# Pacing of the last gathers of R in a dense stage: by the matmuls of the stage, or by the transposes and products that follow it

## The chip, the cores and the metric

The kernel runs on one core of a Trainium2 chip. The metric is the device time of one execution in microseconds (us), as the median of several runs. A profile of one execution was taken as well. The engines are called PE (TensorE; its weight loads are PEld), DVE (VectorE), ACT (ScalarE), POOL (GpSimd) and SP (SyncE).

## The reference

The inputs are x (8 batches, 2048 nodes, 128 features) and a symmetric-pattern matrix adj (2048 x 2048) of which about 0.4% is not zero. Two layers follow each other, each with a residual sum and a layer norm:

```
res = si[:, :, None] + sj[:, None, :] + adj * w_r + g_b        # si, sj = x @ parts of g_w
X1  = layernorm(x + einsum('bij,bjd->bid', res, x) @ weight + bias)

x1 = einsum('bnf,nw->bwf', X1, adj);  x2 = 2 * einsum(x1, adj) - X1    # the same adj twice
out = layernorm(X1 + relu(concat([X1, x1, x2, x1, x2]) @ Theta1 + bias))
```

In the first layer the sums with si, sj and g_b have rank 9 and are added by small matmuls; what costs is adj times Y, with Y = w_r * (x @ weight). In the second layer the products with Theta1 are taken first, so that two hops remain: y = X1 @ T1 + adj^T @ U with U = X1 @ T0, and then X1 @ T2 + adj^T @ y.

## The kernel before

The 2048 nodes are 16 chunks of 128. In the first layer the first three chunks (0, 1, 2) are computed densely: for each, PE multiplies the transposed rows of adj (in `wide`) with all sixteen chunks of Y (L862). The thirteen others are computed from lists. While chunks 1 and 2 are multiplied, DVE finds for each of these chunks which of the 2048 nodes have a non-zero entry: one list for each quarter of 32 rows ("quads"), one for each half of 64 and one for the whole chunk, at most 128 nodes in each. Seven lists make one chunk. The order of these chunks is `seq` = 9, 10, 11, 12, 13, 14, 3, 4, 5, 6, 7, 8, 15.

For each list two things are gathered by POOL, in 128 rows, by `gather` (L656 to L666, profile line L659). The first is R: rows of the chunk's columns of adj and of its transpose, 1 KB a row, from `rr_d` into one of four buffers `stage`. The second is Y: rows of 4 KB from `y0_d` (y_d in the profile) into a ring of nine buffers that are named Y in the profile, as are the chunks of Y. A quad set of R has four gathers, the set of halves and whole three. The list `jobs` (L699 to L705) holds the order of all gathers of R: ten quad sets for seq[0] to seq[9], then the set of three for chunk 9, the quads of chunk 7, the set of three for chunk 10, the set of three for chunk 11, and so on.

`gathers(count, mm)` (L709) issues the next `count` of these jobs. With a matmul `mm` each of these gathers waits, by a semaphore, for that matmul. At the start of a set, when three sets are waiting, the oldest is copied by DVE (`keep_r`, L687 and L693) out of its stage buffer into `rc` and `rct`, where the matmuls of listed rows (L894) take their weights. `keep_r` is pinned behind whatever DVE instruction was traced before it. Every gather is tied behind the one traced before it:

```
        if order:
            behind(g, order[-1])
        order.append(g)
```

so POOL's order is the order in which the program is written. The rest is placed by a compile-time scheduler, except what is pinned in program order (SP's loads) or tied behind the last matmul by `in_order` (list `mms`).

In the loop over the dense chunks, `c` is the chunk that is finished and chunk c + 1 is multiplied in sixteen steps j. `finish0` adds x, and `layernorm` gives X1. `make_u` (L388) transposes X1 (PE, L184, eight transposes), copies the transposes (DVE L176, ACT L178), stores X1^T (ACT queue, L396), multiplies it into U (PE, L402, eight products in two halves), copies U (ACT, L407) and stores it (L408). At the end of c = 1 this is done for chunk 0, at the end of c = 2 for chunk 1. Y gathers of chunk 9 (seven) and the first two of chunk 10 are issued at j = 9 to 13 of c = 1, with three gathers of R between them at j = 11.

Then the loop over `seq` begins: the own block of a chunk (L878), `put` (the chunk's R is copied out of its stage buffers), the R gathers of the next chunk, and the listed rows (L894) with the Y gathers that are still missing, each of which waits for its ring buffer.

Of the kernel before, what the change touches and what calls it, by code (L numbers as in the profile page):

```python
# [18 lines left out]
def kernel(  # L19
# [86 lines left out]
    def rows4(name):  # L106
        return w4.tile([P, B, D], F32, name=name, tag="w4")

    def flat(t):
        return t.rearrange("p b f -> p (b f)")  # L110
# [69 lines left out]
    def transpose4(srcs, name, t=None, dve=None, tie=None):  # L180

        pt = p_tr.tile([P, 4, P], F32, name=f"pt_{name}", tag="pt")
        for i, s in enumerate(srcs):
            mm = nc.tensor.transpose(pt[:, i, :], s, ident)  # L184
            if tie is not None:
                tie(mm)
        if t is None:
            t = trp.tile([P, 4, P], F32, name=f"tr_{name}", tag="tr")
        evict(t, pt, dve)
        return t  # L190
# [42 lines left out]
    def load_x(c, name, q, t=None):  # L233
        if t is None:
            t = rows4(f"{name}{c}")
        tc.keep_in_program_order(
            q.dma_start(out=t, in_=x[:, c * P:(c + 1) * P, :].rearrange("b p f -> p b f"))
        )
        return t
# [127 lines left out]
    def acc_pair():  # L367
        par[0] ^= 1
        return bank[2 * par[0]:2 * par[0] + 2]
# [18 lines left out]
    def make_u(c, z, xt, u=None, tie=None, mid=None):  # L388

        for h in range(2):  # L390
            transpose4([z[:, h * HB + i, :] for i in range(4)], f"p{c}_{h}",
                       xt[:, h * HB:(h + 1) * HB, :], tie=tie)
        if mid is not None:
            mid()
        if c < ND:
            nc.scalar.dma_start(out=xt_d[c], in_=flat(xt))  # L396
        if u is None:
            u = rows4(f"u{c}")
        for h in range(2):
            pp = p_sm.tile([P, HB, D], F32, name=f"pp{c}_{h}", tag="sm")  # L400
            for i in range(HB):
                mm = nc.tensor.matmul(  # L402
                    pp[:, i, :], xt[:, h * HB + i, :], th[:, 0, :], start=True, stop=True
                )
                if tie is not None:
                    tie(mm)
            nc.scalar.copy(u[:, h * HB:(h + 1) * HB, :], pp)  # L407
        nc.scalar.dma_start(out=u_d[c * P:(c + 1) * P, :], in_=flat(u))  # L408

    def copy_r(n0, n1):  # L410
        for c in seq[n0:n1]:
            tc.keep_in_program_order(
                nc.sync.dma_start(out=rr_d[c - ND][0:N, 1, :], in_=adj[:, c * P:(c + 1) * P])
            )
# [225 lines left out]
    def tile_lists_end():  # L640
        return lists_end(0, LP, [(h, 0, lists[:, 0:64], 64 * h, NT) for h in range(2)])
# [29 lines left out]
    def gather_r(c, q, m, st, n):  # L671


        gather(
            st[:, n * m * P:(n + 1) * m * P],
            rr_d[c - ND].rearrange("n m f -> n (m f)") if m == 2 else adj128,
            idx if m == 2 else idr,
            4 * c + n if q else (LP + 2 * c, LP + 2 * c + 1, LF + c)[n], NX if m == 2 else N * NC,
        )

    def keep_r(c, q, m, st):

        for o in range(m):
            out = rc[:, c] if o == m - 1 else rct[:, c - ND]
            n, w, o1, a = (4, TW, 0, 0) if q else (2, 2 * TW, P, LP)
            step = m * P + w
            tc.keep_in_program_order(nc.vector.tensor_mul(  # L687
                out[:, o1:o1 + P].rearrange("p (n f) -> p n f", n=n),
                st[:, 0:n * step].rearrange("p (n f) -> p n f", n=n)[:, :, o * P:o * P + w],
                has[:, a + n * c:a + n * c + n][:, :, None].to_broadcast([P, n, w]),  # L690
            ))
            if not q:
                tc.keep_in_program_order(nc.vector.tensor_scalar(  # L693
                    out[:, 2 * P:3 * P], st[:, (2 * m + o) * P:(2 * m + o + 1) * P],
                    has[:, LF + c:LF + c + 1], None, op0=ALU.mult,
                ))
# [12 lines left out]
    def gathers(count, mm=None):  # L709

        for _ in range(count):
            if not jobs:
                break
            c, q, n = jobs.pop(0)
            if n == 0:
                if len(waiting) == 3:
                    keep_r(*waiting.pop(0))
                waiting.append((
                    c, q, int(c >= ND) + 1,
                    stages[:, turn[1] % 4 * BD:turn[1] % 4 * BD + BD + 4 * TW],  # L720
                ))
                turn[1] += 1
            gather_r(*waiting[-1], n)
            if mm is not None:
                tc.add_manual_dep(
                    order[-1].ins, mm.ins.name,
                    mybir.DependencyInfo(
                        mybir.DependencyClass.Sync, mybir.DependencyReason.DATA
                    ), reason="pace",
                )  # L730
# [70 lines left out]
    mms = []  # L801
# [7 lines left out]
    with nc.allow_non_contiguous_dma(reason="512-byte rows of blocks"):  # L809
        pending, accs, xr = None, acc0, load_x(0, "xr", nc.sync)  # L810
        for c in range(ND):
            if c + 1 < ND:
                xr1 = load_x(c + 1, "xr", nc.sync)
            if c == 0:
                more_rows()
                copy_r(2, 9)
                tile_ranks()
                tile_lists()
                half_ranks()
                make_ub()  # L820
                for n in range(NC):
                    tc.keep_in_program_order(
                        nc.sync.dma_start(out=y0_d[n * P:(n + 1) * P, :], in_=flat(Y[n]))
                    )
                copy_r(9, NC - ND)
                tc.keep_in_program_order(nc.sync.dma_start(out=y0_d[N:, :], in_=flat(ub)))
                at = tile_lists_end()
                chunk_ranks()
                rank1(0, accs, si_t(0))
                mm = None  # L830
            else:
                z = finish0(c, accs, xr, c > 1)
            if c + 1 < ND:
                accs1, sit, at1 = acc_pair(), si_t(c + 1), first_at[c + 1]
                for j in range(NC):
                    if c == 0:
                        if j < 2:
                            candidates(2 * j)
                            candidates(2 * j + 1)
                        if j == 2:  # L840
                            z = finish0(c, accs, xr, False)
                            layernorm(z, "0_0", at)
                        if j > 4 and j % 2:
                            list_round((j - 5) // 2)
                    else:
                        if j in (1, 3):
                            list_round((j + 11) // 2)
                        if j == 11:
                            made, at = chunk_lists_end()
                            layernorm(z, "0_1", at)  # L850
                            fetch_own(0, y0_d, seq[0])
                            late0 = fetch_block(0, seq[0])
                    if c == 0:
                        gathers(2, mm)
                    elif j < 3 or j in (11, 14, 15):
                        gathers((2, 2, 1)[j] if j < 3 else 3 if j == 11 else 2, mm)
                    elif 9 <= j < 13:
                        fetch_lists(0, y0_d, seq[0], {9: 2, 10: 4, 12: 7}[j])
                    elif j == 13:
                        fetch_lists(0, y0_d, seq[1], NG4 - 7)  # L860
                    for h in range(2):
                        mm = nc.tensor.matmul(  # L862
                            accs1[h], at1[:, j, :], Y[j][:, h * HB:(h + 1) * HB, :],
                            start=(j == 0), stop=False, skip_group_check=True,
                        )
                        if c == 1 and j == 11:
                            behind(mm, made)
                rank1(c + 1, accs1, sit)
                if c == 0:
                    gathers(3, mm)  # L870
                accs = accs1
            if pending is not None:
                make_u(*pending, tie=in_order)
            pending, xr = (c, z, rows4(f"xt{c}")), xr1

    def block_rows(t, r, accs, start, stop):
# [214 lines left out]
```

## Time and profile before

| what | value |
|---|---|
| median of 3 runs | 855.61 us (852.25 to 860.12) |
| the profiled execution, its own time | 867.91 us |
| its span, first to last instruction | 866.1 us |
| PE busy | 748.5 us (86%) |
| POOL busy | 430.1 us (50%) |
| DVE busy | 364.1 us (42%) |
| gathers of R from rr_d (L659) | 91, mean 1035 ns |
| gathers of Y from y_d (L659) | 203, mean 994 ns |
| DMA, mean over the span | 311 GB/s |

Starts and durations are in us from the first instruction. In a line of the order of time, the brackets give the idle time of the engine ahead of the instruction and what ended it; "issue" is time in which it waited for nothing that the profile shows. In a table by stage, each engine has its busy time and in parentheses its instructions, and the last three columns are PE's granted clock, the DMA engines' busy share and what they moved in GB/s.

### The profile page before, as it was taken

What the parts mean: (1) busy time and instruction counts of PE and PEld (TensorE: products, weight loads), DVE (VectorE), ACT (ScalarE), POOL (GpSimd) and SP (SyncE); (2) the same over time, 40 slices, a digit from 0 to 9 for tenths busy, and PEclk for the clock granted to TensorE, in tenths of its full rate; (3) what the DMA queues carried; (4) which work ended last, traced back from release to release, by engine and by line L of the source; (5) the groups of instructions that cost most, each with busy time, mean ns of one, the idle gap of its engine ahead of it and who ended that gap; (6) DMA issues with size and microseconds to landing.
All of it is one profiled execution on the core that took longest, in us unless ns stands there. A gap on an engine that the chain in (4) does not pass through costs nothing.

```text
span 866.1 us, 10670 instructions
## 1 busy us (share of the span) xinstructions
PE 748.5 (86%) x3546; PEld 373.8 (43%) x3546; DVE 364.1 (42%) x1062; ACT 175.1 (20%) x428; POOL 430.1 (50%) x438
## 2 busy tenths in 40 slices
PE   5899999998829778498996987989999899999994
PEld 4666665643324333153344442333343444445541
DVE  5555667769523335155353010000100046555666
ACT  3665664010011212021222000000000002011111
POOL 0000000277466676657675456766655656566660
PEclk9999999999869998799998999999999999999998
DMA  8699997799968889979997889999998989999994
GB/s 283 194 306 309 342 303 215 231 373 398 287 212 264 268 274 322 368 250 344 342 363 259 280 314 349 315 341 394 383 365 307 322 290 372 350 341 354 342 350 155
DMA packets 177548, 269.19 MB, mean 311 GB/s; under 512 B 17698, under 2 KB 127701, under 8 KB 175438
## 3 DMA queue, kind: packets, MB, share of 16 engines
q0 software_dynamic: 50400, 151.21, 49.0%
q1 hardware_dynamic: 103900, 90.02, 32.0%
q10 hardware_dynamic: 23186, 27.20, 8.8%
q8 instruction: 30, 0.49, 0.2%
q14 instruction: 32, 0.26, 0.1%
HBM read 246.75 MB, written 62.55 MB: 357 GB/s over the span
## 4 chain that ended last, share of the span: by engine, by line
PE 53%; DMA 19%; issue 10%; another core or an unknown queue 8%; POOL 3%; DVE 3%; ACT 2%; POOLq 1%; SPq 0%; DVEq 0%; ACTq 0%
PE acc L894 19%; DMA Y<-u_d,idx 9%; DMA Y<-y_d,idx 9%; PE acc L862 7%; PE acc L878 5%; PE acc L342 4%; PE acc L332 4%; PE acc L952 3%; POOL Y L659 3%; PE pt_a L184 2%; PE pp L402 2%; DMA rc<-in_adj_dram 1%; PE pt_x L184 1%; PE pt_r L970 1%
## 5 line engine op out<-in xcount | busy, mean ns | idle before, releaser
L659 POOL DMA_INDIRECT Y<-y_d,idx x203 | 201.8, 994 | 134.7 <-PE acc L894 72.4
L894 PE MATMUL acc<-Y,rc 128*32 128x512 f32 (+2 forms) x896 | 222.3, 612 | 21.9 <-DMA Y<-u_d,idx 11.7
L659 POOL DMA_INDIRECT stage<-rr_d,idx x91 | 94.2, 1035 | 199.8 <-PE rank_c L514 164.4
L659 POOL DMA_INDIRECT Y<-u_d,idx x112 | 111.4, 994 | 69.8 <-PE acc L894 35.5
L894 PEld LDWEIGHTS acc<-Y,rc 128*32 128x32 f32 (+2 forms) x896 | 59.5, 129 | 174.5 <-issue 107.0
L894 PE MATMUL acc<-Y,rct 128*32 128x512 f32 (+2 forms) x364 | 106.2, 621 | 18.6 <-issue 14.0
L878 PE MATMUL acc<-Y,rd 128*128 128x512 f32 x148 | 70.0, 594 | 0.8 <-issue 0.8
L894 PEld LDWEIGHTS acc<-Y,rct 128*32 128x32 f32 (+2 forms) x364 | 25.5, 129 | 90.4 <-issue 67.5
L862 PE MATMUL acc<-Y,wide 128*128 128x512 f32 x128 | 59.9, 620 | 4.3 <-issue 4.3
L383 DVE TENSOR_TENSOR xs<-acc,xs 128x512 f32<-128x512 f32 x26 | 17.8, 684 | 103.8 <-PE acc L894 59.8
L176 DVE COPY z<-acc 128x512 f32<-128x512 f32 x9 | 6.2, 692 | 115.7 <-issue 41.0
L219 ACT ACTIVATE st<-st,epst 128x8 f32<-128x8 f32 x32 | 10.0, 311 | 210.1 <-DVE st L218 112.8
L184 PE MATMUL pt_a<-ident,rc 128*128 128x128 f32 x256 | 37.6, 282 | 6.4 <-DMA rc<-in_adj_dram 6.0
L972 DVE SCALAR_TENSOR_TENSOR z<-z,pt_r 128x512 f32<-128x512 f32 x32 | 20.5, 684 | 47.0 <-PE acc L894 28.5
L862 PEld LDWEIGHTS acc<-Y,wide 128*128 128x128 f32 x128 | 24.7, 199 | 34.5 <-issue 34.4
L311 DVE TENSOR_REDUCE stage<-rct 128x64 f32<-128x2048 f32 x13 | 29.7, 2286 | 23.1 <-ACT rct L178 23.1
L332 PE MATMUL acc<-wx,tr_x 128*128 128x130 f32 x256 | 36.5, 286 | 3.2 <-ACT tr_x L178 2.8
L303 DVE TENSOR_REDUCE rc<-rc 128x64 f32<-128x2048 f32 x16 | 36.5, 2278 | 6.3 <-DMA rc<-in_adj_dram 6.3
L332 PEld LDWEIGHTS acc<-wx,tr_x 128*128 128x128 f32 x256 | 32.8, 194 | 13.4 <-ACT tr_x L178 5.9
L184 PEld LDWEIGHTS pt_a<-ident,rc 128*128 128x128 f32 x256 | 30.9, 145 | 16.3 <-issue 14.7
L342 PE MATMUL acc<-Y,wide 128*128 128x512 f32 x64 | 36.0, 645 | 1.7 <-ACT Y L336 0.5
L407 ACT COPY u<-pp 128x512 f32<-128x512 f32 x30 | 17.5, 585 | 98.3 <-PE acc L894 58.7
(221 smaller groups left out, 895.2 us busy)
## 6 DMA issues: line engine op xcount, KB each, us to landing
rc<-in_adj_dram SPq DMA_DIRECT2D x16, 1024.0 KB
rr_d<-rct SPq DMA_DIRECT2D x13, 1024.0 KB
rr_d<-in_adj_dram SPq DMA_DIRECT2D x13, 1024.0 KB
xs<-in_x_dram SPq DMA_DIRECT2D x21, 512.0 KB
y_d<-Y SPq DMA_DIRECT2D x16, 512.0 KB
out_dram<-z ACTq DMA_DIRECT2D x16, 512.0 KB
u_d<-u ACTq DMA_DIRECT2D x15, 512.0 KB
Y<-y_d SPq DMA_DIRECT2D x15, 512.0 KB
```

Of the source, the lines that this page charges most:

```text
L184: mm = nc.tensor.transpose(pt[:, i, :], s, ident)
L303: nc.vector.tensor_reduce(mk[:, c, :], a.rearrange("p (w f) -> p w f", f=TW), AX.X, ALU.max, apply_absolute_value=True,)
L311: nc.vector.tensor_reduce(mkt[:, :, 4 * c:4 * c + 4], at.rearrange("p j (t f) -> p j t f", f=TW), AX.X, ALU.max, apply_absolute_value=True,)
L332: nc.tensor.matmul(py[:, i, 0:D + 2], xt[b // HB][:, (b + i) % HB, :], wx, start=True, stop=True,)
L342: nc.tensor.matmul(acc0[h], first_at[0][:, c, :], Y[c][:, h * HB:(h + 1) * HB, :], start=(c == 0), stop=False, skip_group_check=True,)
L383: nc.vector.tensor_add(xr[:, hs, :], accs[h], xr[:, hs, :])
L659: g = nc.gpsimd.indirect_dma_start(out=out, out_offset=None, in_=src, in_offset=bass.IndirectOffsetOnAxis(ap=ids[:, n:n + 1], axis=0), bou ...
L862: mm = nc.tensor.matmul(accs1[h], at1[:, j, :], Y[j][:, h * HB:(h + 1) * HB, :], start=(j == 0), stop=False, skip_group_check=True,)
L878: in_order(nc.tensor.matmul(accs[h], r, t[:, h * HB:(h + 1) * HB, :], start=start, stop=stop, skip_group_check=True,))
L894: in_order(nc.tensor.matmul(accs[h][w * t:w * t + w], r[:, o + w * t:o + w * t + w], gs[t][:, h * HB * D:(h + 1) * HB * D], start=False, s ...
L952: in_order(nc.tensor.matmul(accs[h][:, b, :], x1t[c][:, h * HB + b, :], th[:, i, :], start=(b == 0), stop=False, skip_group_check=True,))
L972: nc.vector.scalar_tensor_tensor(z[:, hs, :], z[:, hs, :], 0.0, pt, op0=ALU.max, op1=ALU.add)
```

## The change

In the step c = 1 the gathers of R at j = 14 and j = 15 (two each, waiting for a dense matmul) are taken out. After each `make_u` in this loop, that is for chunk 0 and for chunk 1, four gathers of R are issued: two wait for the last of the eight transposes (`mms[-9]`), two for the last product of U (`mms[-1]`). So eight gathers stand where four stood; the four that are added here are taken from the next chunks' sets, which issue four fewer later on.

```
@@ -852,8 +852,8 @@
                     if c == 0:
                         gathers(2, mm)
-                    elif j < 3 or j in (11, 14, 15):
-                        gathers((2, 2, 1)[j] if j < 3 else 3 if j == 11 else 2, mm)
+                    elif j < 3 or j == 11:
+                        gathers((2, 2, 1)[j] if j < 3 else 3, mm)
                     elif 9 <= j < 13:
                         fetch_lists(0, y0_d, seq[0], {9: 2, 10: 4, 12: 7}[j])
@@ -871,6 +871,8 @@
             if pending is not None:
                 make_u(*pending, tie=in_order)
+                gathers(2, mms[-9])
+                gathers(2, mms[-1])
             pending, xr = (c, z, rows4(f"xt{c}")), xr1
```

More of the change, by code (lines that the diff above doesn't have):

```diff
@@ L854 @@
                         gathers(2, mm)
-                    elif j < 3 or j in (11, 14, 15):
-                        gathers((2, 2, 1)[j] if j < 3 else 3 if j == 11 else 2, mm)
+                    elif j < 3 or j == 11:
+                        gathers((2, 2, 1)[j] if j < 3 else 3, mm)
                     elif 9 <= j < 13:
@@ L873 @@
                 make_u(*pending, tie=in_order)
+                gathers(2, mms[-9])
+                gathers(2, mms[-1])
             pending, xr = (c, z, rows4(f"xt{c}")), xr1
```

## The prediction

> **What bounds the kernel now.** I read the page first, then the chain of waits over 195 to 330 us, then the order of time of each engine around the place of the change, and last the table by stage.
>
> ```profile
> span 866.1 us, 10670 instructions
> PE 748.5 (86%) x3546; PEld 373.8 (43%) x3546; DVE 364.1 (42%) x1062; ACT 175.1 (20%) x428; POOL 430.1 (50%) x438
> L659 POOL DMA_INDIRECT stage<-rr_d,idx x91 | 94.2, 1035 | 199.8 <-PE rank_c L514 164.4
> ```
>
> No engine is full over the whole span, so the stage decides. The 91 gathers of R (tile stage) are issued one at a time by POOL. The chain shows what the end of the dense stage hangs on:
>
> ```profile
> 224.65 10.21 PE acc L862 x20
> 240.15 16.55 another core or an unknown queue
> 257.56 4.11 PE pp L402 x16
> 261.67 3.48 PE acc L878 x8
> 265.14 5.64 PE acc L894 x28
> ```
>
> The reader is to see that dense matmuls (L862) lead until 235, that in this execution something takes 16.55 us out of the chain, and that the U of chunk 1 (L402), the own blocks (L878) and the first listed rows (L894) follow. POOL is not in the chain here. The order of time on POOL and PE:
>
> ```profile
> 229.64 0.99 POOL L659 DMA_INDIRECT Y<-y_d,idx  x1 [6.70 <-issue]
> 234.84 1.00 POOL L659 DMA_INDIRECT stage<-rr_d,idx  x1 [0.30 <-issue]
> 238.76 1.00 POOL L659 DMA_INDIRECT Y<-y_d,idx  x1 [0.30 <-issue]
> 245.26 1.01 POOL L659 DMA_INDIRECT stage<-rr_d,idx  x1 [0.30 <-issue]
> 247.88 1.00 POOL L659 DMA_INDIRECT stage<-rr_d,idx  x1 [0.30 <-issue]
> 250.50 1.00 POOL L659 DMA_INDIRECT stage<-rr_d,idx  x1 [0.31 <-issue]
> 253.11 1.00 POOL L659 DMA_INDIRECT stage<-rr_d,idx  x1 [0.30 <-issue]
> 258.23 1.12 POOL L659 DMA_INDIRECT stage<-rr_d,idx  x1 [4.12 <-DVE rc L687]
> 267.25 0.99 POOL L659 DMA_INDIRECT Y<-y_d,idx  x1 [5.23 <-PE acc L894]
> 236.70 1.09 PE L184 MATMUL pt_p<-ident,xr 128*128 128x128 f32 x8
> 238.21 2.05 PE L402 MATMUL pp<-th,xt 128*128 128x128 f32 x16 [0.42 <-DVE xt L176]
> 240.10 1.04 PE L184 MATMUL pt_p<-ident,xr 128*128 128x128 f32 x8
> 255.26 0.59 ACT L407 COPY u<-pp 128x512 f32<-128x512 f32 x1 [7.91 <-remote]
> 250.00:255.00 5.00, 0.00 (x0) 0.00 (x0) 0.00 (x0) 0.00 (x0) 3.19 (x4) 0.50 0.27 76
> ```
>
> From 229.64 to 254.11 POOL issues 19 gathers in a row, each 1.00 us with 0.30 us ahead of it: 1.30 us a gather. "Issue" there means that no semaphore held it. So POOL is bound by its own issue, not by the waits that pace it. The first wait of another kind is at 267.25, where a Y gather waits for a listed-rows matmul that frees its buffer. The last line (busy time by engine, clock, DMA share, GB/s) shows the DMA engines at 0.27 and PE idle at half clock.
>
> **What the Trainium skill says.** "DMA: Bandwidth & Descriptors", section "Anatomy of one DMA — SWDGE (gpsimd) path": DMA engines do not wait on semaphores, the wait sits on the issuing sequencer. So a paced gather holds everything behind it on POOL; the trace agrees, POOL stands 5.23 us before 267.25. "Perfetto Trace Analysis", section "DMA Instruction — SWDGE (GPSIMD)": the profiled end of such a DMA is when its descriptors are written, not when data has landed; so 1.00 us is issue alone, and the semaphore record for the gather issued at 250.50 shows the landing at 253.07, 2.57 us on. The same DMA page, "Queues, rings and completion order": each DMA engine takes the queues in turn, packet by packet; late R gathers thus share with row loads; no view here separates that share. "TensorE: Matmul & The Clock Gate", "What's actually happening": after an idle window of about 3.4 us the array runs at half clock; the table shows 0.50 from 250 to 255.
>
> **The change, part by part.** Number the gathers of R by chunk: R7 (4, quads), R10 (3), R11 (3). Before: R7 at j = 14 and 15, paced by dense matmuls; R10 after the own blocks of chunk 9 begin; R11 one step later. After: R7 in two pairs, behind X1^T and behind U of chunk 0; then R10 and the first R11 in two pairs, behind X1^T and U of chunk 1; two R11 remain.
>
> 1. *POOL's order.* Every gather is tied behind the one traced before it, so the order on POOL is the traced order. Before: 5 Y, R7 x4, R10 x3, R11 x3, Y of chunk 10. After: the same list. No gather is added or removed, none overtakes a Y. Cost 0.
>
> 2. *The old waits.* The two dense matmuls end before 235; R7 begins at 245.26. They held nothing: gain 0.
>
> 3. *The new waits, PE in time.* X1^T of chunk 0 ends at 236.70 + 1.09 = 237.8; U of chunk 0 at 238.21 + 2.05 = 240.3; X1^T of chunk 1 at 240.10 + 1.04 = 241.1. U of chunk 1, without the hole of 16.55 us, follows after two copies of X1^T; with 0.84 us from copy to first matmul (256.72 to 257.56), 2.05 us of matmuls as for chunk 0, and an estimate of 0.6 us for the second copy behind ACT's queue (one 0.59 us copy), it ends at 241.1 + 0.84 + 2.05 + 0.6 = 244.6. POOL reaches the four pairs at 245.26, 247.88, 250.50 and 253.11 for the first of each. Slack 7.5, 7.6, 9.4 and 8.5 us. Nothing waits. Cost 0; the cover is the run of Y gathers ahead, and it would be gone if PE ran 8 us late.
>
> 4. *The new waits, PE late as in this execution.* ACT's second copy of U of chunk 0 starts at 255.26 when its matmuls count as done, and U of chunk 1 ends at 257.56 + 4.11 = 261.67. Then R7's third goes at 255.3 instead of 247.88, its fourth at 256.6, R10's first two at 257.9 and 259.2, its third waits for 261.7, R11 follow at 263.0, 264.3 and 265.6, and POOL is free at 265.6 + 1.0 + 0.3 = 266.9. Behind it is the Y gather of chunk 10, which before could not go until 267.25 because of the listed rows. Slack 0.3 us: delay 0. This holds whenever PE is late, because four gathers (5.2 us) run against PE's own 3.48 us of own blocks plus its first listed rows, 261.67 to 267.12 = 5.45 us.
>
> 5. *Who needs the late R.* R10 is copied by DVE (L687, L693) for chunk 10 at 276.27; its last gather, issued at 261.7, would land with the 4.7 us that the gather of 258.23 took (262.89) at 266.4. Ten us of cover. R11 is used a chunk later, R7 much later. Cost 0.
>
> 6. *DMA load.* In case 4 two to three R gathers (at most 128 rows of 1 KB, 0.13 MB each) move from before 264 to the stretch in which Y of chunk 10 lands. 0.39 MB at the page's mean of 311 GB/s is 1.3 us; the engines are 66 to 88% busy there, so the bounds are 0 and 1.3 us on Y. PE waits for these Y at 279 to 286, so it can reach the path. I take 0.7.
>
> 7. *DVE and the buffers.* Each new set makes the oldest of three waiting sets be copied out. One set of quads moves from DVE's idle time at 230.3 to behind the copy of X1^T at 238.2: two instructions, about 0.2 us apart, 0.4 us on the statistics of chunk 2, whose product is not transposed until 270.6. The other two stay behind the copy of X1^T of chunk 1, as at 257.43. Cost 0, upper bound 0.4. SP's loads and ACT's stores are neither moved nor added. A wait word on POOL costs some 0.05 us under a running gather.
>
> *Sum.* PE in time: 0. PE late: +0.7 (0 to 1.7). Against the profiled execution's own 867.91 us (span 866.1 and 1.8 around it) that is 867.9 to 869.6. It carries the hole and lies 12.3 us above the median of the runs, 855.61; the change in us is carried over to the median unchanged, since neither case scales with the run.
>
> **Rivals.** *The waits bind but are hidden* (step 4): 855.6 + 0.7 = 856.3. For it: the profiled hole. Against: it needs PE more than 7.5 us behind POOL.
>
> *Slower: the last wait backs up into chunk 10.* If U of chunk 1 is late and POOL's remaining gathers take longer than 1.30 us each (one at 276.36 took 1.48), the Y of chunk 10 starts late. Price: with six R gathers still ahead when POOL is let go, 6 x 1.30 = 7.8 instead of 5.45 us gives +2.4; six R of 0.13 MB in front at 311 GB/s give +2.5; and when the PE gaps at 279 to 286 join into one over 3.4 us, half clock adds up to the 4.1 - 2.05 = 2.1 us per 16-matmul U and likewise for listed rows, an estimate of 4 to 5 us for one chunk. Together about +9.4: 865. It decides from a Y start later than 268 on. Against it: step 4's race comes out even by construction.
>
> *Faster: less traffic beside the Y of chunks 9 and 10 and the stores of X1^T and U.* At most 7 x 0.13 MB at 311 GB/s = 2.9 us: 852.7; a fall past 1% would also need the compiler's plan, which sees the R later, to place the untied DVE and ACT work better: 846 as an estimate. Against: the stretch 250 to 255 has the DMA engines at 0.27, so there is no queue to relieve, and the hole starts at 240.15, before the first R at 245.26.
>
> **How the numbers follow.** Nothing binds: 0.58, 855.6. Binds and is hidden: 0.22, 856.3. Backs up: 0.13, 865. Faster: 0.07, 846. The two likeliest differ by less than can be measured (about 1%), so one figure: 856. Faster by over 1% 0.07, within 1% 0.80, slower by over 1% 0.13. The range holds the two middle cases, the 0 to 1.7 us of step 6 and 7, the spread of the runs (852.25 to 860.12), and reaches to the backed-up case: 849 to 865.
>
> **What would show it.** Right: POOL's list in the same order, R7 starting some 16 us after the first Y gather, with "issue" ahead of R7 and R10, or, with PE late, a wait on PE L184 or L402 ahead of them and the first Y of chunk 10 still waiting on PE L894. Wrong: that Y gather starting right behind an R gather at "issue" after a POOL wait on L402, listed rows of chunk 10 waiting longer for Y, or a POOL order other than the one listed.

## The result and the profile after

Beside each other on one chip, the kernel before takes 859.24 us (852.25 to 866.30) and the kernel after 855.05 us (851.62 to 861.47), medians of 20 runs each. The ratio on record is 0.9975, with an interval of 0.9952 to 0.9998: 0.25% faster, some 2 us, where no change was forecast (856, range 849 to 865). The two medians lie 4.2 us apart, so the size is known only roughly. The gain is smaller than the 1% that the chances speak of, and about as large as what the kernel before later strays from itself (1.0021), so this comparison alone doesn't settle that there is one. Ratios are of fast runs, and the profiled execution before (867.91 us) is a slow one, but a fast one of the same kernel (e5_control below, 861.27 us) has the same hole.

The profiled execution after took 853.63 us, with a span of 851.9. Its page:

```profile
span 851.9 us, 10671 instructions
PE 754.3 (89%) x3546; PEld 374.6 (44%) x3546; DVE 364.4 (43%) x1062; ACT 174.8 (21%) x428; POOL 427.3 (50%) x438
L659 POOL DMA_INDIRECT stage<-rr_d,idx x91 | 92.5, 1016 | 198.2 <-PE rank_c L514 163.9
```

The same number of instructions on every engine, the same 91 gathers of R. Nothing was saved in work, so a gain has to come from waits. The chain of waits of the kernel after, in the stretch of which the prediction showed five lines (line numbers are two higher than before: L896 is the old L894, L880 the old L878):

```profile
220.18 9.42 PE acc L862 x20
235.66 5.69 another core or an unknown queue
242.21 2.05 PE pp L402 x8
244.26 4.79 issue
249.04 2.08 PE pp L402 x8
251.12 4.01 PE acc L880 x8
255.13 4.79 PE acc L896 x26
```

Before, one piece of 16.55 us stood between the dense matmuls and U of chunk 1. After, there are two, 5.69 and 4.79 us. In the order of time of POOL, PE, DVE and ACT the place looks so (the brackets: idle before, and what ended it); the last line is from the table by stage:

```profile
229.25 0.99 POOL L659 DMA_INDIRECT Y<-y_d,idx  x1 [6.78 <-ACT xr L225]
244.84 1.00 POOL L659 DMA_INDIRECT stage<-rr_d,idx  x1 [0.30 <-issue]
250.07 1.00 POOL L659 DMA_INDIRECT stage<-rr_d,idx  x1 [0.31 <-issue]
255.07 0.99 POOL L659 DMA_INDIRECT stage<-rr_d,idx  x1 [2.70 <-PE acc L880]
260.27 1.00 POOL L659 DMA_INDIRECT Y<-y_d,idx  x1 [0.30 <-PE acc L896]
231.44 1.09 PE L184 MATMUL pt_p<-ident,xr 128*128 128x128 f32 x8
233.17 0.30 DVE L687 TENSOR_TENSOR rct<-stage,has 128x128 f32<-128x128 f32 x1
241.37 0.69 DVE L176 COPY xt<-pt_p 128x512 f32<-128x512 f32 x1 [5.71 <-remote]
254.74 0.58 ACT L407 COPY u<-pp 128x512 f32<-128x512 f32 x1 [5.75 <-PE acc L880]
250.00:255.00 5.00, 5.00 (x14) 2.54 (x12) 0.00 (x0) 0.26 (x1) 2.00 (x2) 0.78 0.43 150
```

R7 starts at 244.84 with "issue" ahead of it, so its waits bind nothing here. The third gather of R10 stands 2.70 us for U of chunk 1. Y of chunk 10 follows R11 without a gap. PE, which had no busy time from 250 to 255, now fills these 5 us. From the first transpose of chunk 0 (231.44) to the end of U of chunk 1 (251.12) it is 19.7 us; before it was 236.70 to 261.67, 25.0 us. Below, this length is called the stretch. One thing in these lines is easily read over: in the profile after, the stretch ends at 251.12, before POOL's first wait for PE begins (255.07 - 2.70 = 252.37), and DVE's copy of X1^T of chunk 1 comes at 241.37 in the middle of POOL's run. So that wait didn't make the stretch of this pair shorter; what did is open.

### The profile page after: what moved, and what is told of

Same layout as the page of the kernel before. It is cut to its first block, busy times and chain, and to the rows that moved or that the text cites. A ratio compares the mean times of both kernels' runs of the same rounds, so it can differ in the third digit from the quotient of the medians.

```text
span 851.9 us, 10671 instructions
## 1 busy us (share of the span) xinstructions
PE 754.3 (89%) x3546; PEld 374.6 (44%) x3546; DVE 364.4 (43%) x1062; ACT 174.8 (21%) x428; POOL 427.3 (50%) x438
## 4 chain that ended last, share of the span: by engine, by line
PE 54%; DMA 25%; issue 11%; POOL 4%; ACT 3%; DVE 1%; another core or an unknown queue 1%; POOLq 1%; SPq 0%; DVEq 0%; ACTq 0%
PE acc L896 19%; DMA Y<-y_d,idx 13%; DMA Y<-u_d,idx 10%; PE acc L862 7%; PE acc L880 6%; PE acc L342 4%; PE acc L954 4%; PE acc L332 4%; POOL Y L659 3%; PE pp L402 2%; PE pt_a L184 2%; DMA rc<-in_adj_dram 1%; PE pt_x L184 1%; PE pt_p L184 1%; PE pt_r L972 1%
## 5 line engine op out<-in xcount | busy, mean ns | idle before, releaser
L896 PE MATMUL acc<-Y,rc 128*32 128x512 f32 (+2 forms) x896 | 226.5, 608 | 18.7 <-issue 7.6
L896 PEld LDWEIGHTS acc<-Y,rc 128*32 128x32 f32 (+2 forms) x896 | 59.2, 128 | 175.7 <-issue 113.7
L896 PE MATMUL acc<-Y,rct 128*32 128x512 f32 (+2 forms) x364 | 108.5, 625 | 26.4 <-issue 13.1
L880 PE MATMUL acc<-Y,rd 128*128 128x512 f32 x148 | 72.0, 610 | 0.0
L896 PEld LDWEIGHTS acc<-Y,rct 128*32 128x32 f32 (+2 forms) x364 | 27.0, 130 | 96.2 <-issue 71.5
```

The costliest lines, as they stand in the source:

```text
L880: in_order(nc.tensor.matmul(accs[h], r, t[:, h * HB:(h + 1) * HB, :], start=start, stop=stop, skip_group_check=True,))
L896: in_order(nc.tensor.matmul(accs[h][w * t:w * t + w], r[:, o + w * t:o + w * t + w], gs[t][:, h * HB * D:(h + 1) * HB * D], start=False, s ...
```

## The experiments

The theory that stood after this comparison: the waits give the gain, by something that they do to the late results of PE (theory W). Rivals: DVE's moved copy gives it (theory D); it is chance (theory N). Every kernel ran beside the kernel before on the same chip. The five sets differ in one thing that turned out to matter: what the kernel before itself took.

| set | before, us | kernel | ratio (95%) | stretch, us | POOL's first pause, us | PE's results from, us |
|---|---|---|---|---|---|---|
| record | 859.24 | before | | 25.0 | 254.11 | 256.72 |
| | | after | 0.9975 (0.9952 to 0.9998) | 19.7 | 252.37 | 254.74 |
| first | 830.55 | e1_order | 1.0010 (0.9991 to 1.0028) | 12.5 | | |
| | | e2_waits | 0.9994 (0.9969 to 1.0020) | 9.7 | | |
| | | e3_hold | 1.0018 (1.0003 to 1.0033) | 8.3 | | |
| | | e4_again | 0.9991 (0.9972 to 1.0009) | 14.9 | | |
| second | 863.87 | e5_control | 1.0021 (0.9997 to 1.0045) | 23.7 | 254.45 | 256.12 |
| | | e6_again | 0.9916 (0.9892 to 0.9940) | 14.9 | 242.25 | 245.51 |
| | | e7_waits | 0.9988 (0.9960 to 1.0016) | 21.8 | 249.90 | 252.31 |
| | | e8_early | 1.0017 (0.9991 to 1.0042) | 25.7 | 249.41 | 252.35 |
| third | 858.37 | e9_order | 1.0025 (1.0003 to 1.0048) | 23.0 | 250.64 | 253.08 |
| | | e10_r7 | 0.9976 (0.9941 to 1.0012) | 16.9 | 246.97 | 249.05 |
| | | e11_y | 0.9988 (0.9956 to 1.0020) | 22.2 | 248.20 | 249.24 |
| | | e12_late | 1.0005 (0.9979 to 1.0031) | 18.0 | 248.72 | 250.66 |
| fourth | 862.63 | e13_sp | 0.9937 (0.9906 to 0.9967) | 14.3 | 243.65 | 245.55 |
| | | e14_again | 0.9950 (0.9925 to 0.9974) | 17.9 | 247.23 | 249.40 |
| | | e15_r7 | 1.0006 (0.9974 to 1.0038) | 15.0 | 242.40 | 244.39 |
| | | e16_both | 1.0000 (0.9970 to 1.0029) | 16.0 | 244.88 | 247.19 |
| fifth | 830.92 | e17_hold | 1.0005 (0.9983 to 1.0028) | 12.2 | | |
| | | e18_again | 1.0032 (1.0006 to 1.0058) | 10.4 | | |

The pause is the first idle time of POOL over 1 us after the first Y gather: the start of the gather behind it less the idle time in its bracket. The last column is the start of DVE's first step on results of PE behind the pause (in the profile after, where DVE's came earlier, ACT's copy of U). By this definition the last column lies behind the pause; what the table can show is how close behind, and that it moves with the pause. Against it stand late results that came while POOL was still issuing, in at least ten of the fourteen profiles: the first half of U of chunk 0 in seven of them, 0.8 to 10.4 us ahead of the pause (246.76 in the kernel before), and three copies in the profile after. Stretch, pause and copy are of one profiled execution each; the ratios are of many runs.

**First set: the parts of the change.** e1_order is the change without its waits:

```
-                gathers(2, mms[-9])
-                gathers(2, mms[-1])
+                gathers(2)
+                gathers(2)
```

> The changed kernel without its waits: the eight gathers of R stand after U of chunks 0 and 1, tied to no matmul. POOL's order and DVE's order are those of the changed kernel, so only one copy of a quad set is moved on DVE and no wait is added. If the waits bring the 0.25%, the ratio to before is 1.000 (within 0.002). If the moved copy on DVE brings it, 0.9975. If the difference measured was chance, 1.000. In its profile POOL runs from the first Y gather to the last R gather without a stop but for the stage buffers (R11 waiting for DVE).

e2_waits is the kernel before with only the waits of R10 and R11's first gather:

```
             make_u(*pending, tie=in_order)
+            if c == 2:
+                gathers(2, mms[-9])
+                gathers(2, mms[-1])
```

> The kernel before with the waits alone: R7 stays at j = 14 and 15 with its dense matmuls, and R10 with the first R11 stands after U of chunk 1, two behind its X1^T and two behind its U. The copies on DVE stay where they were before. If the waits bring the 0.25%, 0.9975; if the moved copy brings it, 1.000; if chance, 1.000. In its profile POOL stops ahead of the third R10 until U of chunk 1 is done, as in the changed kernel (2.70 us there).

e3_hold puts eight gathers behind U of chunk 1 (`if c == 2: gathers(8, mms[-1])` in place of the two calls):

> All eight gathers of R wait for the last product of U of chunk 1. If a POOL that stands still lets PE finish X1^T and U sooner, the stretch from the first transpose of chunk 0 to the last U of chunk 1 shrinks from 24.97 us (before) and 19.7 us (changed) to about 13 us, nearly what the matmuls and copies need. Behind that U POOL then has ten gathers of R (13 us) ahead of the Y of chunk 10, against 5.45 us of PE's own work: Y starts about 7.6 us later than PE could use it. Relief theory: the two offset, 0.995 to 1.003. Back-up rival without relief: up to 7.6 us slower, 1.005 to 1.009.

e4_again is the kernel after:

> The changed kernel once more, beside the others on the same chip: 0.9975 if its gain is real (interval 0.9952 to 0.9998 so far), 1.000 if it was chance.

All four are within 0.2% of before, the whole change too (e3_hold is 0.18% slower, with an interval that just leaves out 1). The trace shows why. In e1_order neither copy of U of chunk 1 is late, in the order of time of ACT:

```profile
235.63 0.58 ACT L407 COPY u<-pp 128x512 f32<-128x512 f32 x1 [4.20 <-PE pp L402]
242.25 0.58 ACT L407 COPY u<-pp 128x512 f32<-128x512 f32 x1 [0.77 <-PE pp L402]
```

The last product of U of chunk 1 is done at 242.2, before POOL comes to R7 at 245.64; no wait for it could have bound. The longest stretch of the set, 14.9 us in e4_again, holds one late copy, for which PE waits 5.11 us, and ends before R7 as well. POOL issues its gathers at the same times as in the profiled kernel before, yet PE's results come promptly. That is the case "PE in time" of the prediction's step 3, and it gives what step 3 says, nothing. The kernel before takes 29 us less here than beside the result: this set could not show the gain at all.

**Second set: PE is late again.** e5_control is the kernel before; e6_again the kernel after; e7_waits is e2_waits again. e8_early brings R7 forward into POOL's idle time ahead of the first Y gather:

```
-    sets = [(c, True) for c in seq[:10]]
+    sets = [(c, True) for c in seq[:11]]
-        if n in (0, 2, 4):
+        if n in (2, 4):
-                    elif j < 3 or j in (11, 14, 15):
-                        gathers((2, 2, 1)[j] if j < 3 else 3 if j == 11 else 2, mm)
+                    elif j < 5 or j == 11:
+                        gathers((2, 2, 1, 2, 2)[j] if j < 5 else 3, mm)
```

> The kernel before, unchanged, against itself. Every theory expects a ratio of 1 with an interval of about 0.002 to each side; its middle shows how far a comparison strays with no change at all. Its trace is read for one thing: whether the stretch from the first transpose of chunk 0 to the end of U of chunk 1 is long (25 us, as in the profiled kernel before) or short (8 to 15 us, as in the four kernels of the first set).

> The kernel after, again. If the gain of 0.25% comes from the waits while PE is late, it appears (0.996 to 0.999) where this run's stretch is long and POOL waits for U of chunk 1 (2.70 us in the profile after), and not where the stretch is short (0.999 to 1.001). If it comes from the copy that DVE does later, it appears in both. If it was chance, the ratio is within 0.002 of 1 whatever the stretch.

> The kernel before, with R7 paced by the dense matmuls as it was, and only the four gathers behind make_u of chunk 1 tied to the transposes and the products of U. If the wait for U of chunk 1 gives the gain, this has all of it where PE is late: 0.996 to 0.999. If DVE's order gives it, this has none: 1.000.

> The kernel before with the four gathers of R7 at j = 3 and 4 of the step c = 1, ahead of the Y gathers, in the 6 us in which POOL stood idle before the first Y gather (5.96 us at 230.06 in the first set's profile of the order alone). Theory that POOL's issue bounds the first listed chunks: the ten gathers ahead of the first free Y gather of chunk 10 become six, that Y starts up to 4 x 1.30 = 5.2 us sooner, and the kernel is 2 to 5 us faster (0.994 to 0.998). Rival, that the Y gather waits for its buffer, which the listed rows of chunk 9 free, or that the R of later chunks only moves the wait: 0.999 to 1.001. If the earlier R holds up the first Y gathers behind it, 1.002 or more.

e5_control has the hole of the kernel before again:

```profile
257.63 1.00 POOL L659 DMA_INDIRECT stage<-rr_d,idx  x1 [3.18 <-DVE rc L687]
256.12 0.69 DVE L176 COPY xt<-pt_p 128x512 f32<-128x512 f32 x1 [15.26 <-remote]
```

The control strays to 1.0021, and the kernel after gains 0.84%: theory N falls. e7_waits has little or none of it. e8_early, which should have helped a POOL-bound chunk 10, gains nothing. The traces of this set gave the theory that the rest of the study tests. First the kernel after (e6_again), the order of time of POOL and DVE:

```profile
246.04 1.00 POOL L659 DMA_INDIRECT stage<-rr_d,idx  x1 [3.79 <-remote]
251.83 1.00 POOL L659 DMA_INDIRECT stage<-rr_d,idx  x1 [3.48 <-PE pp L402]
237.77 0.21 DVE L221 RECIPROCAL st<-st 128x8 f32<-128x8 f32 x1 [2.99 <-issue]
245.51 0.69 DVE L383 TENSOR_TENSOR xr<-acc,xr 128x512 f32<-128x512 f32 x1 [3.47 <-remote]
```

Here R7's waits do bind, twice. POOL has issued gathers without a break since 216.45 and stands still from 242.25; 3.3 us later the first result of PE arrives at DVE. During POOL's run the hand-over between DVE and ACT in the layer norm is slow as well: L221 waits 2.99 us for ACT where the kernel before has 0.38. The delay thus lies in part ahead of the stretch, which begins at 241.66 here and at 235.31 in e7_waits: U of chunk 1 ends at 256.52, only 0.6 us sooner than in e7_waits (257.07), though the stretch is 6.9 us shorter and no gain of e7_waits is shown. Now e8_early, DVE and POOL:

```profile
230.76 0.21 DVE L630 TENSOR_SCALAR rct<-pl 128x48 f32<-128x48 f32 x1 [11.18 <-remote]
252.35 0.69 DVE L383 TENSOR_TENSOR xr<-acc,xr 128x512 f32<-128x512 f32 x1 [13.32 <-remote]
260.81 1.00 POOL L659 DMA_INDIRECT stage<-rr_d,idx  x1 [11.40 <-DVE rc L687]
```

Filling POOL's idle 6 us came with a second wait, 11.18 us where the profiled kernel before has 4.51 (without this move e15_r7 has 9.03, so the move isn't shown to be its cause), and the old one ends 2.9 us after POOL's pause (260.81 - 11.40 = 249.41). Hence theory P: where PE's results are late, they come when POOL stops issuing gathers, and the waits of the change make it stop sooner.

**Third set: theory P.** e9_order is e1_order again. e10_r7 has the calls behind `make_u` under `if c == 1`, so only R7 waits. e11_y takes j = 12 and 13 out of the lists fetched in step c = 1 and has, behind `make_u` of chunk 0:

```
+                if c == 1:
+                    n = len(order)
+                    fetch_lists(0, y0_d, seq[0], 7)
+                    fetch_lists(0, y0_d, seq[1], NG4 - 7)
...
+                        order[n].ins, mms[-9].ins.name,
```

e12_late is the kernel before without the calls at j = 14 and 15 and with the later quad sets at `n in (3, 5, 7)`, no wait added.

> The kernel after without its waits: the same order on every engine, four gathers behind make_u of chunk 0 and of chunk 1, none of them waiting for PE. Theory P (a pause of POOL): what PE, DVE and ACT signal to each other arrives late for as long as POOL issues gathers without a break, and the waits of R7 break that run early, at about 242 to 245 us instead of 250 to 254. Then this has none of the gain: 0.998 to 1.002, and on a chip where PE is late, its first results after the run come 2 to 3 us after POOL's first pause, not before 250 us. Theory D (DVE's order): all of the gain, 0.992 to 0.997. On a chip where PE is not late, both give 1.000.

> The kernel after with the four gathers behind make_u of chunk 0 alone (R7, waiting for X1^T and U of chunk 0), and nothing behind make_u of chunk 1. Theory P, where PE is late: all of the gain of the whole change, 0.991 to 0.998, with POOL waiting for PE ahead of R7 (3.79 us in the second set's run of the kernel after). If the gain needs the second wait too, 0.998 to 1.000. Where PE is not late: 1.000.

> The kernel after with the pause put earlier: the last three Y gathers of chunk 9 and the two of chunk 10 are moved behind make_u of chunk 0 as well, and the first of them waits for its transposes. Theory P, where PE is late: POOL pauses at about 237 to 239 us instead of 242 to 245, chunk 0's results come some 5 us sooner, and U of chunk 1 ends before 250 us: 0.988 to 0.994, better than the kernel after. Rival: Y of chunk 9 now comes late and the listed rows of chunk 9 wait for it by what the pause takes, 2 to 4 us: 1.000 to 1.004; on a chip where PE is not late this rival is what theory P expects too, at 1.000 to 1.002.

> The kernel before with the four gathers of R7 left out of this place, without any wait on PE: R7 follows three sets later (and the quads of chunks 6 and 8, or what stands there in the list, likewise), when POOL is past the stage. POOL's unbroken run is four gathers, 5.2 us, shorter. Theory P, where PE is late: PE's results after the run come about 5 us sooner (251 instead of 256 us), 0.994 to 0.998. Theory that only a wait on PE helps: 0.999 to 1.001. Where PE is not late: four gathers fewer ahead of Y of chunk 10 are worth 0 to 3 us there and are paid back later, 0.997 to 1.001.

e9_order speaks between W and D. Order of time, POOL, ACT and DVE:

```profile
254.87 0.99 POOL L659 DMA_INDIRECT stage<-rr_d,idx  x1 [4.23 <-DVE rc L687]
253.02 0.59 ACT L407 COPY u<-pp 128x512 f32<-128x512 f32 x1 [6.42 <-remote]
253.08 0.69 DVE L176 COPY xt<-pt_p 128x512 f32<-128x512 f32 x1 [13.90 <-remote]
```

Every engine has the order of the kernel after, no gather waits for PE, PE is late, and there is no gain (1.0025). That speaks against D, but the kernel after itself didn't run in this set; the fourth set completes it. POOL pauses first at 250.64, and both copies start 2.4 us later. In e12_late, POOL and DVE:

```profile
252.81 1.00 POOL L659 DMA_INDIRECT stage<-rr_d,idx  x1 [4.09 <-DVE rc L687]
250.66 0.69 DVE L176 COPY xt<-pt_p 128x512 f32<-128x512 f32 x1 [8.95 <-remote]
```

Here no PE wait is added and POOL's run is only shorter: the pause moves to 248.72, the copy to 250.66, the stretch to 18.0 us, as P says, and yet the time is 1.0005. e11_y missed its aim: the transposes of chunk 0 were not late in its profile (POOL first stood at 248.20), and the time did not move. e10_r7 lies where the whole change lay at first, with an interval that holds 1.

**Fourth set: POOL's issue or the bytes.** e13_sp loads R7 and R10 by SP's queue instead of by POOL. The loads take as many rows, but not those of the lists, so only its time can be compared:

```
+        if (c, q) in ((seq[10], True), (seq[1], False)):
+            load = tc.keep_in_program_order(nc.sync.dma_start(
+                out=st[:, n * m * P:(n + 1) * m * P],
+                in_=rr_d[c - ND].rearrange("n m f -> n (m f)")[n * P:(n + 1) * P],
+            ))
...
+            return
```

e14_again is the kernel after, e15_r7 is e10_r7, and e16_both joins the kernel after with e12_late's later sets (`gathers(1, mms[-1])` in the second call).

> The kernel before, but the seven gathers of R7 and R10 are plain loads of the same 128 rows of 1 KB each by SP's queue, the first of them waiting for the last Y gather in front to land; the rows are not those of the lists, so the products of these two sets are not the reference's. Bytes and buffers stay, POOL's unbroken run ends with the second Y gather of chunk 10, at about 245 us. Theory P (POOL's issue): where PE is late, the copies of U of chunk 0 and of X1^T of chunk 1 come at 246 to 248 us instead of 252 to 257, 1 to 3 us after POOL's pause. Theory T (the transfers): POOL's pause changes nothing, the copies come when the R loads have moved, from 252 us on. Time: P 0.994 to 0.999, T 0.999 to 1.003; SP's own loads stand behind the R loads, which may cost 1 to 3 us in either case.

> The kernel after, again. Theory P: 0.991 to 0.998 where the stretch of the kernels without waits is long, with POOL waiting for PE at R7 or at R10; 0.999 to 1.001 where it is short.

> R7's waits alone, again. Theory P with the first pause deciding: the same ratio as the kernel after of this set within 0.002. If the second wait, for U of chunk 1, adds to it: 0.002 or more behind the kernel after, and 1.000 if it gives all.

> Both: R7 follows three sets later, R10 waits for X1^T and U of chunk 0 (two gathers and one), R11 for X1^T and U of chunk 1. POOL's first pause is where the kernel after has it, and four gathers fewer stand ahead of Y of chunk 10. If POOL's issue is what chunk 10 waits for, 0.003 better than the kernel after of this set; if its Y waits for the listed rows of chunk 9, as 1.70 us on PE L896 in the second set's run of the kernel after says, the same as that kernel within 0.002.

e13_sp is faster by 0.63%. POOL and DVE, and two lines of its table by stage (busy time by engine, PE's clock, DMA share, GB/s):

```profile
252.25 1.00 POOL L659 DMA_INDIRECT stage<-rr_d,idx  x1 [8.60 <-DVE rc L700]
245.55 0.69 DVE L176 COPY xt<-pt_p 128x512 f32<-128x512 f32 x1 [1.29 <-remote]
243.00:246.00 3.00, 0.00 (x0) 0.00 (x0) 1.68 (x4) 0.39 (x1) 0.66 (x1) 0.58 0.86 294
246.00:249.00 3.00, 2.71 (x12) 2.71 (x13) 2.19 (x13) 0.78 (x2) 0.00 (x0) 0.50 0.74 300
```

POOL pauses at 243.65 and the copy starts at 245.55, while the DMA engines are at 0.86 and move 294 GB/s; the R loads are issued only at 248.67. In the kernel before it was the reverse: from 250 to 255 the DMA engines were at 0.27, POOL was issuing for most of it, and the results were still out. In e5_control they were out at 0.80 (245 to 250) and in e9_order at 0.26 (247 to 250). So the load of the DMA engines is not what holds PE's results. POOL's issue, or something that goes with it, fits; the transfers of the gathers themselves go with it, and no run separates the two. As in e12_late, no wait on PE was needed to shorten the stretch. The 0.63% can't be put down to that alone, since POOL also has seven gathers less to issue.

The kernel after gains 0.50% in this set. R7's wait alone (e15_r7) and both waits with R7 placed later (e16_both) gain nothing, although their stretches, 15.0 and 16.0 us, are shorter than the 17.9 of the kernel after. That speaks against a simple sum in which each us of the stretch reaches the end. e15_r7 also tells on D: it has DVE's moved copy, behind the copy of X1^T of chunk 0 (244.39), and no gain in a set in which the kernel after has one:

```profile
244.99 0.28 DVE L687 TENSOR_TENSOR rct<-stage,has 128x128 f32<-128x128 f32 x1
```

So D falls: the moved copy by itself gives no gain. But e16_both has both waits and no gain either, so theory W isn't shown: waits and a shorter stretch aren't enough.

**Fifth set.** e17_hold is e3_hold and e18_again the kernel after.

> The kernel of e3_hold again: nothing behind make_u of chunk 0, eight gathers behind make_u of chunk 1, all waiting for the last product of its U. Where PE is late, theory P: POOL pauses with the last Y gather at about 244 us and stays still until U of chunk 1, which ends 250 us or sooner, the shortest stretch of all kernels; if a shorter stretch is what the time follows, 0.991 to 0.996. Rival: all ten gathers then stand ahead of Y of chunk 10, which starts 13 us after U of chunk 1, later than the listed rows of chunk 9 (5.5 us) would let it, and gives the gain back: 0.998 to 1.004. Where PE is not late: 1.002, as measured in the first set.

> The kernel after, again, as the yardstick of this set: 0.991 to 0.998 where the stretch of 15 us or more is seen, 0.999 to 1.001 where it is 8 to 13 us.

The kernel before takes 830.92 us here, the stretches are 12.2 and 10.4 us, and the question put to this pair could not be answered: there was no lateness to shorten. What it adds is the other side: with PE in time the kernel after is not faster (1.0032, with an interval just above 1; 0.9991 in the first set).

## Why the prediction was wrong, step by step

- **Steps 1 and 2 held.** POOL's list is the same, and the old waits held nothing. But one line was misread ahead of them: "the first wait of another kind is at 267.25" passes over the gather of 258.23, ahead of which POOL stands 4.12 us, from 254.11, for a copy of DVE. It is beside this pause that PE's late results come (255.26 and 256.72).
- **Step 3 held where it applies.** With PE in time nothing binds. Against a predicted 0, one set measured 0.9991, and the other 1.0032, some 2.7 us slower and just clear of 1; the kernel before has strayed from itself by 0.21% (e5_control), so this isn't shown to be a cost of the waits.
- **Step 4 held in what it says of POOL**: with PE late, a wait binds (2.70 us in the profile after) and Y of chunk 10 is not delayed by it. In the profile after the race came out as even as computed, with Y right behind R11 at 260.27.
- **The step that failed is what step 4 takes as given.** It let POOL's list run against PE's times of the profiled kernel before, with ACT's second copy at 255.26 "when its matmuls count as done", as if these times did not depend on POOL. The profiles say that they do, at least in part. In fourteen profiles with PE late, POOL's first pause lay anywhere from 242.25 to 254.45, and the next result of PE that DVE took (in the profile after, ACT) came 1.0 to 3.3 us behind it; where POOL's run was cut short with no wait on PE, results came sooner too (e12_late, e13_sp). A wait that makes POOL stop can then end a delay, where step 4 counted only what it costs. So the term "PE late: +0.7 (0 to 1.7)" had the wrong sign: 0.9975, 0.9916 and 0.9950 are -2, -7 and -4 us. That the waits gain by this pause is argued only; in the profile after, the stretch was shorter before POOL paused at all.
- **The faster rival was refused on facts that did not decide.** The DMA engines stand at 0.27 in that profile, but at 0.70 from 250 to 255 in e5_control. Its mechanism, less traffic, isn't what brought the results in e13_sp, where they came at 0.86. "The hole starts at 240.15, before the first R at 245.26" is true, but the start of the hole says nothing on its end, and POOL's run had begun with the Y gathers at 229.64.
- **The weights were off too.** "Nothing binds" had 0.58 because PE more than 7.5 us late was taken as the exception. In four of the six sets every profile had PE late.
- **Step 7 held**: DVE's moved copy stands at 233.17, behind the copy of X1^T, and e9_order and e15_r7, which have it too, gain nothing. Step 6 was not measured by itself.

What was known already and underrated: the Trainium skill, "Perfetto Trace Analysis", section "Tensor Engine Instruction (MATMUL, LD_WEIGHTS)", says that a matmul's end in the profile is estimated from the instruction's size, and that the semaphore update, sent when PSUM has acknowledged the write, comes after it, outside the time that the profile gives for the matmul. The trace agrees: U of chunk 0 starts at 238.21 for 2.05 us by the records before, and its two halves are copied at 246.76 and 255.26. The modelled end told nothing about when others could go on. The trace also keeps records of the semaphores themselves: in e5_control, updates by PE stand at 243.99, 250.41 and 256.09 us, each 0.02 to 0.03 us ahead of the copy that waited for it (244.01, 250.43 and 256.12). So it is PE's signal that came late, and not the engine that took it.

Two things stay open. Why the results are late at all: POOL issues the same gathers when the kernel takes 831 us, and hardly anything is late; the first and the third set ran on the same chip, so it isn't the chip alone. And how the gain gets from the stretch to the end. From the first transpose of chunk 0 to the end of the span, the profiles with PE late and no added wait (before, e5_control, e8_early, e9_order, e12_late) took 629.4, 622.1, 625.4, 619.1 and 621.4 us; those of the kernel after 620.5, 616.8 and 622.5. The means, 623.5 and 619.9, differ by less than single profiles scatter (10 us), and e15_r7 and e16_both, without a gain, took 618.2 and 621.0, so these profiles don't show where the gain lies. Nor is the place of the change all that is slow: behind U of chunk 1 the fourteen profiles with PE late took 596 to 608 us to the end, the six others 588 to 592. e12_late, e15_r7 and e16_both shortened the stretch without a gain that their intervals of 0.3% show, so the shorter stretch is shown, and that it is the gain is argued only.

## What to carry to other kernels

When a profile has a hole that no instruction explains, don't hold its times fixed while moving another engine's work: look at which queue runs without a break through it, and whether the hole ends when that queue stops. A wait that is "free" on paper may act by the pause that it makes; whether that reaches the end of the kernel has to be measured by itself. And measure in more than one setting: the same kernel stood at 831 and at 864 us, and the change is worth nothing in one and 0.2 to 0.8% in the settings of 858 us and more, where it was measured.

## What the runs showed of the hardware that was not expected

- The unchanged kernel before had medians of 830.55, 830.92, 858.37, 859.24, 862.63 and 863.87 us in the six sets. The late results go with the four slower ones.
- In those, the copy of X1^T came as much as 16.2 us (e8_early, 237.66 to 253.88) and 16.6 us (before, chunk 1, 240.10 to 256.72) behind the recorded start of its transposes, against 0.8 us in chunk 0 of before (236.70 to 237.48), and a DVE to ACT to DVE hand-over of 0.38 us (before) took 2.99 us (e6_again) while POOL issued gathers.
- An indirect gather of 128 rows mostly took POOL 1.00 us, with 0.30 us ahead of it, whether the rows have 1 KB (before, 234.84) or 4 KB (before, 238.76).
